# Layer 1 scans: a projection in two passes, copies on ScalarE instead of VectorE, and new costs for the order planner

## The chip, the cores and the metric

The kernel runs on one core of a Trainium2 chip. Five engines work beside each other[...]: TensorE (PE in the profile, PEld for its weight loads), VectorE (DVE), ScalarE (ACT), GpSimd (POOL) and SyncE (SP), which here issues all DMAs. [...] The metric is device time of one execution in microseconds (us), lower is better; the number compared is the median over runs.

## The reference

Two layers on x of shape (4, 128, 128, 192), float32. Each layer is x + block(groupnorm(x)). Layer 0's block has a state space scan with one state and dilated convolutions; it isn't touched here. Layer 1's block, cut to what matters:

```
xz = x @ in_proj_w;  x_ssm, z = halves          # C = 192
xc = silu(depthwise 3x3 conv(x_ssm) + conv_b)
xs = [xc row-major, reversed, column-major, reversed]      # K = 4 directions
proj  = xs @ x_proj_w[k]                        # 12 + 16 + 16 columns: dpart, B, C
delta = softplus(dpart @ dt_w[k] + 2 dt_b[k])
for t in 0 .. L-1:                              # L = 128 * 128
    state = exp(delta_t * A) * state + (delta_t * xs_t) * B_t      # 16 states a channel
    y_t   = sum over states of state * C_t
y = sum over k of (y_k + Ds * xs_k), each put back into image order
out = layernorm(y) * silu(z) @ out_w
```

The recurrence over 16,384 positions, for 4 images, 4 directions, 192 channels and 16 states, is most of the arithmetic. It is the part of the kernel that the change is in.

## The kernel before

The function `scans` handles two images at a time (a pair) as three blocks of 128 partitions: channels 0 to 127 of the first image, the last 64 channels of both, channels 0 to 127 of the second. Positions go in tiles of T = 1024. A *step* is one pair, one direction k and one tile: 2 x 4 x 16 = 128 steps. In a step there are six *groups* m of 64 channels (x = 0 to 5), and in a group eight *units* q, each of 64 channels times two states on 128 partitions: 48 units a step, 6,144 in all.

For one step, ahead of its scans:

- `load_u` (L1008) loads the three input blocks `u`.
- `project` makes `pj`, the columns dpart, B and C of both images, in two chunks of 512 positions. PE (L1028) sums three matmuls with 128 x 128 weights, one for each block i, into one PSUM bank; ScalarE copies it out (L1034); SP stores C for later (L1040).
- `step_sizes`, for each block i: two matmuls (L1051) and softplus on ScalarE (L1054) give delta, which goes to HBM (L1058); GpSimd multiplies it into u (L1061); PE transposes that (L1070), and a copy out of PSUM makes `dT` (L1076): on ScalarE for i = 0 and 1, on VectorE for i = 2.
- `diagonals`: for each of the step's two images and four quarters of the tile, two small matmuls transpose a piece of pj (L1094) and VectorE spreads it into a block-diagonal tile `D` (L1100).

For each unit:

- `fill`: eight matmuls (L1174) of 32-row tiles of dT with D make delta * u * B for all eight units of a group, an eighth of the positions at a time; ScalarE evicts them into the ring `H` of 18 slots (L1185). There is one fill buffer in PSUM.
- `unit`: ScalarE makes exp(delta * A) (`dA`, L1201, two buffers in PSUM); VectorE runs the recurrence with a scan instruction, in place in H (L1207); GpSimd multiplies by C (`hc`, L1213, three buffers); PE sums over the states with two 64-column matmuls that write the two halves of a bank (L1221).
- `finish`, after a group's eighth unit: ScalarE keeps the last state (L1237), and VectorE adds the sum to what the earlier direction left, or, for k = 2, which begins a new sum, only copies it out of PSUM (L1243, L1249; L1247 the copy). SP stores it (L1253).

All matmuls of `project`, `step_sizes` and `diagonals` share a single PSUM bank, tag `s`.

The order is not that of the loops. Every piece of work goes to `op(engine, cost, function, reads, writes, ...)` of the class `Order` (from L83). When all are known, `emit` plays them through with a list scheduler: each engine has a time at which it is free, each op a cost in us given by hand, a hop of 0.12 us between engines, 1.28 us for a ScalarE table switch, and DMAs at a given rate. It picks, again and again, the op that can start first; among those that can start within `idle` us of the engine's being free, it picks the one with the lowest rank. The rank is the op's place in the program less its `early`; an op that needs another ScalarE table has `keep` added. What comes out is written down as each engine's instruction order. On the chip the times are what they are; only the order is the planner's.

Of the kernel before, what the change touches and what calls it, by code (L numbers as in the profile page):

```python
# [12 lines left out]
ALU = mybir.AluOpType  # L13
# [187 lines left out]
class Maker:  # L201
# [741 lines left out]
    def scans(self, xc, delta, cs, y, w, ident, alog, dsum, dtb2):  # L943
# [22 lines left out]
        with ExitStack() as ctx:  # L966
# [11 lines left out]

            od = Order(window=3000, keep=1047, idle=0.500, rate=265e3)
            op = od.op  # L980
# [23 lines left out]
            def load_u(s):  # L1004
                p, k, at, j = steps[s]
                for i in range(3):
                    t = us[s, i] = buf("u", 3, 128, T)
                    op("SP", 0.1, lambda t=t, i=i: nc.sync.dma_start(  # L1008
                        t(), xc[k // 2][p][i][:, j * T : (j + 1) * T]
                    ), writes=[t], size=524e3, early=192)  # L1010
                if at == 0:
                    wt = buf("w", 2, 128, 2, 3, 128)
                    op("SP", 0.2, lambda: [
                        nc.sync.dma_start(wt()[:, 0], w["xp1"][:, k]),
                        nc.sync.dma_start(wt()[:, 1], w["dtw1"][:, k]),
                    ], writes=[wt], size=393e3, early=90)
                    wts[p, k] = wt

            def project(s):
                p, k, _, j = steps[s]  # L1020
                wt, uu = wts[p, k], [us[s, i] for i in range(3)]
                t = pj[s] = buf("pj", 1, 128, T)
                for c in range(2):
                    g = bank("P")

                    def mm(g=g, c=c):
                        for i in range(3):
                            nc.tensor.matmul(  # L1028
                                g(), wt()[:, 0, i], uu[i]()[:, 512 * c : 512 * c + 512],
                                start=(i == 0), stop=(i == 2),  # L1030
                            )

                    op("PE", 2.65, mm, reads=[wt, *uu], writes=[g], claims=[t])
                    op("ACT", 0.59, lambda g=g, c=c: nc.scalar.copy(  # L1034
                        t()[:, 512 * c : 512 * c + 512], g()), reads=[g, t], writes=[(t, c)])

                def store():
                    for e in range(2):
                        r = 64 * e + DR + NS
                        nc.sync.dma_start(cs[2 * p + e][k][:, j * T : (j + 1) * T], t()[r : r + NS])  # L1040

                op("SP", 0.2, store, reads=[(t, 0), (t, 1), t], writes=[("cs", s)], size=131e3)

            def step_sizes(s, i):

                p, k, _, j = steps[s]
                wt, u, x = wts[p, k], us[s, i], pj[s]
                l = buf("l", 3, 128, T)
                for c in range(2):
                    g = bank("P")  # L1050
                    op("PE", 0.9, lambda g=g, c=c: nc.tensor.matmul(  # L1051
                        g(), wt()[:, 1, i], x()[:, 512 * c : 512 * c + 512], start=True, stop=True,
                    ), reads=[wt, (x, c), x], writes=[g], claims=[l], early=-123)
                    op("ACT", 0.6, lambda g=g, c=c: nc.scalar.activation(  # L1054
                        l()[:, 512 * c : 512 * c + 512], g(), AF.Softplus,
                        bias=dtb2[:, i % 2, k : k + 1],
                    ), reads=[g], writes=[l], table="softplus")
                op("SP", 0.1, lambda: nc.sync.dma_start(  # L1058
                    delta[p][i][k][:, j * T : (j + 1) * T], l()
                ), reads=[l], writes=[("delta", s, i)], size=524e3)  # L1060
                op("POOL", 2.4, lambda: nc.gpsimd.tensor_tensor(u(), l(), u(), ALU.mult),  # L1061
                   reads=[l], writes=[u], early=30)
                t = dT[s, i] = buf("dT", 4, 128, 2, 8, 64)
                for c in range(2):
                    g = bank("P")

                    def mm(g=g, c=c):
                        for q in range(4):
                            b = 512 * c + 128 * q
                            nc.tensor.transpose(  # L1070
                                g()[:, 128 * q : 128 * q + 128], u()[:, b : b + 128], ident
                            )

                    op("PE", 0.95, mm, reads=[u], writes=[g], claims=[t], early=-249)
                    def turn(copy, g=g, c=c):
                        copy(  # L1076
                            t()[:, :, 4 * c : 4 * c + 4],
                            g().rearrange("t (q h c) -> t h q c", h=2, c=64),
                        )

                    if i < 2:
                        op("ACT", 0.6, lambda turn=turn: turn(nc.scalar.copy), reads=[g], writes=[t], early=-579)
                    else:
                        op("DVE", 0.69, lambda turn=turn: turn(nc.vector.tensor_copy),
                           reads=[g], writes=[t], early=-180)

            def diagonals(s, e, sb):
# [18 lines left out]

                op("PE", 0.4, mm, reads=[(x, sb // 2), x], writes=[g], claims=[t], early=-105)
                op("DVE", 1.2, spread, reads=[g], writes=[t], early=15)
                D[s, e, sb] = t
# [50 lines left out]
            def fill(m, sb, rp):  # L1160
# [19 lines left out]

                op("PE", 1.12, mm, reads=[td, tD], writes=[gs], claims=h[m])

# [8 lines left out]

                op("ACT", 1.13, evict, reads=[gs], writes=h[m])

            def unit(m, q):
# [5 lines left out]
                way = slice(None) if k % 2 == 0 else slice(None, None, -1)  # L1200
                op("ACT", 1.16, lambda: nc.scalar.activation(  # L1201
                    a(), d(), AF.Exp, scale=alog[:, c : c + 1]),
                    reads=[d], writes=[a], table="exp", early=-522)
                s0 = st.get((x, m - 6))

                def scan():
# [4 lines left out]

                op("DVE", 2.34, scan, reads=[a, *([s0] if at else [])], writes=[hq])
                op("POOL", 2.4, lambda: nc.gpsimd.tensor_tensor(t(), hs, tC(), ALU.mult),  # L1213
                   reads=[hq, tC], writes=[t])
                if q == 0:
# [9 lines left out]

                op("PE", 0.95, sum_n, reads=[t], writes=[ym], early=-252)

            def finish(m):
# [12 lines left out]
                def add():  # L1241
                    if k == 0:
                        nc.vector.scalar_tensor_tensor(  # L1243
                            t(), prev[m](), dsum[:, hf : hf + 1], ym(), ALU.mult, ALU.add
                        )
                    elif k == 2:
                        nc.vector.tensor_copy(t(), ym())  # L1247
                    else:
                        nc.vector.tensor_tensor(t(), prev[m](), ym(), ALU.add)  # L1249
# [4 lines left out]

                op("DVE", 0.72, add, reads=[ym, *([prev[m]] if k != 2 else [])], writes=[t])
                op("SP", 0.2, store, reads=[t], writes=[("y", p, k // 2, j, x)], size=262e3)
# [405 lines left out]
```

## Time and profile before

| | us |
|---|---|
| median of 3 runs | 26,409.49 (26,333.76 to 26,457.49) |
| the profiled execution | 26,512.26 |
| its span | 26,510.5 |
| of it, first to last scan of layer 1 | 17,697 (7,208 to 24,906) |

| engine | busy us | share of the span |
|---|---|---|
| PE matmul | 24,193.3 | 91% |
| DVE | 21,935.4 | 83% |
| ACT | 21,016.8 | 79% |
| POOL | 19,902.8 | 75% |

A row of the groups has the line, the engine, the operation, what it writes and reads, the shapes and the count; then the busy time and the mean duration in ns; then the time for which the engine stood idle just before such instructions and what ended most of that. The profile also records the clock that TensorE was granted (PEclk, 1.00 is full). The engines' shares are averages over stages with different limits, and matmul busy time is modelled.

### The profile page before, as it was taken

The page shows a single profiled execution, that of the slowest core. Times are in us where ns is not written, and L with a number is a line of the kernel's source. Part 1 is how long each engine was busy: PE and PEld are TensorE (multiplying, and loading weights), DVE is VectorE, ACT ScalarE, POOL GpSimd, SP SyncE. Part 2 cuts the span into 40 slices and gives each one's busy share as a digit, 9 for nine tenths or more (in the row PEclk, how much of TensorE's full clock was granted, in tenths as well). Part 3 has the DMA queues.
Part 4 walks back from the last instruction along what each step waited for, and adds up shares of the span by engine and source line. Part 5 has one row for each costly group of instructions (what it writes and reads, how often), then busy time and mean ns, then how long its engine had stood idle before and what let it go on. Part 6 is the DMA issues. An engine that isn't in the chain of part 4 may idle for free.

```text
span 26510.5 us, 438073 instructions
## 1 busy us (share of the span) xinstructions
PE 24193.3 (91%) x169220; PEld 9017.9 (34%) x169220; DVE 21935.4 (83%) x15401; ACT 21016.8 (79%) x24359; POOL 19902.8 (75%) x9450
## 2 busy tenths in 40 slices
PE   5999999998799999999999999999999999999699
PEld 3333333332233333333333333333333333333255
DVE  4888888888788889989898888888898888988643
ACT  5988898985588888888888888888888888888433
POOL 3777777763488888888888888888888888888400
PEclk7999999998899999999999899999899999999799
DMA  7999999995544444444444444444444444444573
GB/s 213 242 239 241 242 239 241 239 241 182 185 130 127 133 130 136 135 128 125 117 126 134 126 135 130 130 130 130 125 136 131 117 123 115 133 130 130 182 236 105
DMA packets 1667058, 4220.17 MB, mean 159 GB/s; under 512 B 238545, under 2 KB 387473, under 8 KB 1661905
## 3 DMA queue, kind: packets, MB, share of 16 engines
q1 hardware_dynamic: 1664976, 4192.14, 58.0%
q8 instruction: 1340, 21.95, 0.4%
q14 instruction: 742, 6.07, 0.1%
HBM read 3252.11 MB, written 939.10 MB: 158 GB/s over the span
## 4 chain that ended last, share of the span: by engine, by line
PE 40%; DVE 18%; ACT 11%; issue 6%; DMA 4%; POOL 3%; SPq 0%; DVEq 0%; POOLq 0%; ACTq 0%
DVE h L1207 14%; PE f L1174 13%; PE Y L1221 11%; ACT h L1185 6%; PE s L1028 3%; ACT dA L1201 3%; POOL hc L1213 2%; PE s L1051 2%; DMA C<-cs 2%; PE z L785 1%; PE hf L574 1%; DVE D L1100 1%; DVE acc L896 1%; PE f L785 1%; PE s L1094 1%
## 5 line engine op out<-in xcount | busy, mean ns | idle before, releaser
L1213 POOL TENSOR_TENSOR hc<-h,C 128x1024 f32<-128x1024 f32 x6144 | 14335.4, 2362 | 2412.5 <-PE Y L1221 1154.9
L1207 DVE TENSOR_TENSOR_SCAN h<-dA,st,h 128x1024 f32<-128x1024 f32 x5760 | 13130.9, 2331 | 779.9 <-ACT st L1237 290.6
L1185 ACT COPY h<-f 128x1024 f32<-128x1024 f32 (+3 forms) x8192 | 6332.9, 799 | 2256.1 <-PE f L1174 2185.0
L1174 PE MATMUL f<-D,dT 32*64 32x256 f32 x98304 | 7167.9, 408 | 777.5 <-ACT h L1185 633.6
L1221 PE MATMUL Y<-hc,sel 128*64 128x512 f32 x24576 | 7001.5, 657 | 475.1 <-POOL hc L1213 219.9
L1201 ACT ACTIVATE dA<-d,alog 128x1024 f32<-128x1024 f32 x6144 | 6905.9, 1124 | 301.6 <-DVE h L1207 247.2
L1174 PEld LDWEIGHTS f<-D,dT 32*64 32x64 f32 x98304 | 3279.1, 138 | 6688.2 <-ACT h L1185 4815.8
L452 POOL TENSOR_TENSOR xs<-xs,pr 128x1024 f32<-128x1024 f32 x1536 | 3637.3, 2371 | 329.2 <-ACT pr L447 249.4
L595 DVE SCALAR_TENSOR_TENSOR hf<-hh,vec,hf 128x512 f32<-128x512 f32 x3072 | 2317.8, 755 | 412.9 <-PE hf L574 272.7
L1221 PEld LDWEIGHTS Y<-hc,sel 128*64 128x64 f32 x24576 | 1322.6, 141 | 2979.6 <-issue 1811.3
L574 PE MATMUL hf<-sa,diag 96*32 96x512 f32 x18432 | 2152.3, 600 | 13.2 <-DMA sa<-hpad 11.3
L447 ACT ACTIVATE pr<-xi,vec 128x1024 f32<-128x1024 f32 x1536 | 1713.8, 1143 | 301.1 <-POOL xs L452 296.0
L1100 DVE TENSOR_TENSOR D<-s,mask 128x1024 f32<-128x1024 f32 x1024 | 1238.3, 1209 | 842.0 <-PE s L1094 842.0
L534 POOL TENSOR_TENSOR dl<-dl,xs 128x1024 f32<-128x1024 f32 x192 | 454.7, 2368 | 830.6 <-ACT dA L532 735.5
L574 PEld LDWEIGHTS hf<-sa,diag 96*32 96x32 f32 x18432 | 561.9, 109 | 1479.3 <-issue 1390.5
L1061 POOL TENSOR_TENSOR u<-l,u 128x1024 f32<-128x1024 f32 x384 | 907.2, 2363 | 163.4 <-ACT l L1054 136.0
L1207 DVE TENSOR_TENSOR_SCAN h<-dA,h 128x1024 f32<-128x1024 f32 x384 | 857.1, 2274 | 78.5 <-ACT dA L1201 45.3
L1051 PE MATMUL s<-pj,w 128*128 128x512 f32 x1536 | 892.3, 664 | 7.0 <-ACT l L1054 2.8
L1028 PE MATMUL s<-u,w 128*128 128x512 f32 x1536 | 756.4, 630 | 53.3 <-DMA prev<-xc 52.6
L1054 ACT ACTIVATE l<-s,vec 128x512 f32<-128x512 f32 x768 | 527.8, 687 | 328.5 <-PE s L1051 323.9
L1094 PEld LDWEIGHTS s<-ident,pj 128*128 128x128 f32 x4096 | 554.1, 196 | 599.5 <-issue 256.7
L392 PE MATMUL f<-xa,w 96*128 96x512 f32 (+1 forms) x1536 | 724.8, 616 | 25.7 <-ACT xi L407 25.5
(202 smaller groups left out, 21859.5 us busy)
## 6 DMA issues: line engine op xcount, KB each, us to landing
C<-cs SPq DMA_DIRECT2D x4096, 256.0 KB, 4.7
sa<-hpad SPq DMA_DIRECT2D x2304, 276.0 KB, 7.1
d<-delta SPq DMA_DIRECT2D x1536, 256.0 KB, 4.1
u<-xc SPq DMA_DIRECT2D x384, 512.0 KB, 4.6
delta<-l SPq DMA_DIRECT2D x384, 512.0 KB, 3.6
y<-y SPq DMA_DIRECT2D x1536, 128.0 KB, 3.2
hh<-hpad SPq DMA_DIRECT2D x384, 414.0 KB, 7.7
hpad<-hp SPq DMA_DIRECT2D x192, 552.0 KB, 7.2
```

Of the source, the lines that this page charges most:

```text
L447: op("ACT", 1.1, lambda pr=pr, t=t: nc.scalar.activation(rows(pr()), x()[:, t // 3 : t // 3 + R, t % 3 : t % 3 + W], AF.Copy, scale=v(k, V ...
L452: op("POOL", 2.38, lambda pr=pr: nc.gpsimd.tensor_tensor(o(), o(), pr(), ALU.add), reads=[pr], writes=[o], early=-429)
L574: nc.tensor.matmul(o()[32 * g : 32 * g + 32], diag[:, d, s, k, g], x[:, g, :, c0 : c0 + W], start=(d == 0 and s == 0), stop=(d == 1 and s ...
L595: nc.vector.scalar_tensor_tensor(o3, hh()[:, 1 + dy : 5 + dy, PAD + dx : PAD + dx + W], v(k, V0_K + col), o3, ALU.mult, ALU.add,)
L1028: nc.tensor.matmul(g(), wt()[:, 0, i], uu[i]()[:, 512 * c : 512 * c + 512], start=(i == 0), stop=(i == 2),)
L1100: nc.vector.tensor_tensor(t().rearrange("t a (n s) -> t (a n) s", s=32), g()[:, : 2 * NS].unsqueeze(2).to_broadcast([128, 2 * NS, 32]), ma ...
L1174: nc.tensor.matmul(gs()[64 * jn : 64 * jn + 64, n, 256 * a : 256 * a + 256], td()[rt, r // 64, 2 * sb + a], tD()[rt, a, 256 * jn : 256 * j ...
L1185: nc.scalar.copy(H[:, at : at + nq, 256 * sb : 256 * sb + 256].rearrange("p q (a r s) -> p q a r s", a=2, s=32)[:, :, :, 2 * rp : 2 * rp + 2],
L1201: op("ACT", 1.16, lambda: nc.scalar.activation(a(), d(), AF.Exp, scale=alog[:, c : c + 1]), reads=[d], writes=[a], table="exp", early=-522)
L1207: nc.vector.tensor_tensor_scan(hs[:, way], a()[:, way], hs[:, way], 0.0 if at == 0 else s0()[:, q : q + 1], ALU.mult, ALU.add,)
L1213: op("POOL", 2.4, lambda: nc.gpsimd.tensor_tensor(t(), hs, tC(), ALU.mult), reads=[hq, tC], writes=[t])
L1221: nc.tensor.matmul(ym()[64 * th : 64 * th + 64], sel, t()[:, 512 * th : 512 * th + 512], start=(q == 0), stop=(q == NQ - 1),)
```

## The change

Five things change, all in `scans`:

1. `project` issues, for each chunk, block 1's matmul with all 128 columns first, and then block 0's with columns 0 to 63 and block 2's with columns 64 to 127. Block 0 belongs to the first image and block 2 to the second, so the columns left out multiply by zero weights.
2. In `step_sizes`, the two copies to dT for block 2 go to ScalarE, as those of the other blocks do.
3. In `finish`, the copy for k = 2 goes to ScalarE.
4. The planner's costs are set anew (for instance L1221 from 0.95 to 1.09 us, L1051 from 0.9 to 1.1, the transposes from 0.95 to 1.16, the projection from 2.65 to 2.05), and `keep` and `idle` with them.
5. Many `early` values change: those of the u and weight loads are gone; scans now rank 255 later, exponentials 303 later (522 before), the fills 1,158 earlier, the products with C 1,329 earlier, and the spreads of D no longer 15 earlier.

The order of each of the five engines in this stage follows from all of these.

```diff
-            od = Order(window=3000, keep=1047, idle=0.500, rate=265e3)
+            od = Order(window=3000, keep=869, idle=0.400, rate=265e3)
...
                         t(), xc[k // 2][p][i][:, j * T : (j + 1) * T]
-                    ), writes=[t], size=524e3, early=192)
+                    ), writes=[t], size=524e3)
...
-                    ], writes=[wt], size=393e3, early=90)
+                    ], writes=[wt], size=393e3)
...
-                        for i in range(3):
+                        for i, m in ((1, slice(0, 128)), (0, slice(0, 64)), (2, slice(64, 128))):
                             nc.tensor.matmul(
-                                g(), wt()[:, 0, i], uu[i]()[:, 512 * c : 512 * c + 512],
-                                start=(i == 0), stop=(i == 2),
+                                g()[m], wt()[:, 0, i, m], uu[i]()[:, 512 * c : 512 * c + 512],
+                                start=(i == 1), stop=(i != 1),
                             )
-                    op("PE", 2.65, mm, reads=[wt, *uu], writes=[g], claims=[t])
+                    op("PE", 2.05, mm, reads=[wt, *uu], writes=[g], claims=[t])
...
-                    op("PE", 0.9, lambda g=g, c=c: nc.tensor.matmul(
+                    op("PE", 1.1, lambda g=g, c=c: nc.tensor.matmul(
...
-                    ), reads=[wt, (x, c), x], writes=[g], claims=[l], early=-123)
-                    op("ACT", 0.6, lambda g=g, c=c: nc.scalar.activation(
+                    ), reads=[wt, (x, c), x], writes=[g], claims=[l], early=-189)
+                    op("ACT", 0.69, lambda g=g, c=c: nc.scalar.activation(
...
-                    ), reads=[g], writes=[l], table="softplus")
+                    ), reads=[g], writes=[l], table="softplus", early=378)
...
-                op("POOL", 2.4, lambda: nc.gpsimd.tensor_tensor(u(), l(), u(), ALU.mult),
-                   reads=[l], writes=[u], early=30)
+                op("POOL", 2.38, lambda: nc.gpsimd.tensor_tensor(u(), l(), u(), ALU.mult),
+                   reads=[l], writes=[u])
...
-                    op("PE", 0.95, mm, reads=[u], writes=[g], claims=[t], early=-249)
+                    op("PE", 1.16, mm, reads=[u], writes=[g], claims=[t])
...
-                    if i < 2:
-                        op("ACT", 0.6, lambda turn=turn: turn(nc.scalar.copy), reads=[g], writes=[t], early=-579)
-                    else:
-                        op("DVE", 0.69, lambda turn=turn: turn(nc.vector.tensor_copy),
-                           reads=[g], writes=[t], early=-180)
+                    op("ACT", 0.6, lambda turn=turn: turn(nc.scalar.copy), reads=[g], writes=[t], early=-330)
...
-                op("PE", 0.4, mm, reads=[(x, sb // 2), x], writes=[g], claims=[t], early=-105)
-                op("DVE", 1.2, spread, reads=[g], writes=[t], early=15)
+                op("PE", 0.4, mm, reads=[(x, sb // 2), x], writes=[g], claims=[t], early=-168)
+                op("DVE", 1.2, spread, reads=[g], writes=[t])
...
-                op("PE", 1.12, mm, reads=[td, tD], writes=[gs], claims=h[m])
+                op("PE", 1.1, mm, reads=[td, tD], writes=[gs], claims=h[m], early=1158)
...
-                op("ACT", 1.13, evict, reads=[gs], writes=h[m])
+                op("ACT", 1.05, evict, reads=[gs], writes=h[m])
...
-                op("ACT", 1.16, lambda: nc.scalar.activation(
+                op("ACT", 1.13, lambda: nc.scalar.activation(
...
-                    reads=[d], writes=[a], table="exp", early=-522)
+                    reads=[d], writes=[a], table="exp", early=-303)
...
-                op("DVE", 2.34, scan, reads=[a, *([s0] if at else [])], writes=[hq])
-                op("POOL", 2.4, lambda: nc.gpsimd.tensor_tensor(t(), hs, tC(), ALU.mult),
-                   reads=[hq, tC], writes=[t])
+                op("DVE", 2.34, scan, reads=[a, *([s0] if at else [])], writes=[hq], early=-255)
+                op("POOL", 2.37, lambda: nc.gpsimd.tensor_tensor(t(), hs, tC(), ALU.mult),
+                   reads=[hq, tC], writes=[t], early=1329)
...
-                op("PE", 0.95, sum_n, reads=[t], writes=[ym], early=-252)
+                op("PE", 1.09, sum_n, reads=[t], writes=[ym], early=-270)
...
-                    elif k == 2:
-                        nc.vector.tensor_copy(t(), ym())
...
-                op("DVE", 0.72, add, reads=[ym, *([prev[m]] if k != 2 else [])], writes=[t])
+                if k == 2:
+                    op("ACT", 0.61, lambda: nc.scalar.copy(t(), ym()), reads=[ym], writes=[t])
+                else:
+                    op("DVE", 0.7, add, reads=[ym, prev[m]], writes=[t])
```

## The prediction

> **What bounds the kernel now.** I read the page first, then busy time by stretch, then the groups and the waits of the scans alone, then the timeline. The page's slices show that from slice 11 on four engines run at eight or nine tenths together:
>
> ```profile
> span 26510.5 us, 438073 instructions
> PE   5999999998799999999999999999999999999699
> DVE  4888888888788889989898888888898888988643
> ACT  5988898985588888888888888888888888888433
> POOL 3777777763488888888888888888888888888400
> ```
>
> The first scan begins at 7208 us and the last ends at 24906: 17,697 us for 128 steps, 138.3 each. The change touches nothing else, so the other 8,813 us stay.
>
> Which engine binds depends on the TensorE clock. Busy time by stretch (PE, PEld, DVE, ACT, POOL, clock, DMA share, GB/s), one stretch at full clock and one partly at half:
>
> ```profile
> 18000.00:18100.00 100.00, 92.71 (x776) 34.28 (x772) 93.24 (x49) 87.16 (x113) 89.59 (x39) 1.00 0.53 146
> 18100.00:18200.00 100.00, 97.75 (x563) 33.08 (x562) 66.83 (x35) 57.83 (x58) 57.98 (x26) 0.61 0.33 91
> ```
>
> At full clock VectorE is fullest. At half clock PE is, and everybody waits for it. By the trace's clock records the stage has 94 stretches at half clock, 2,034 us together. Of 127 whole steps, the 54 with a mean clock above 0.985 take 131.6 us, all together 138.2: the half clock costs 6.6 us a step, some 840 us. So this is a kernel bound by VectorE for 89% of the stage and by PE for 11%.
>
> VectorE's work per step, groups of the scans alone (busy, mean ns | idle before):
>
> ```profile
> L1207 DVE TENSOR_TENSOR_SCAN h<-dA,st,h 128x1024 f32<-128x1024 f32 x5760 | 13130.9, 2331 | 779.9 <-ACT st L1237 290.6 <-ACT dA L1201 255.6 <-ACT h L1185 170.2
> L1100 DVE TENSOR_TENSOR D<-s,mask 128x1024 f32<-128x1024 f32 x1019 | 1232.2, 1209 | 805.6 <-PE s L1094 805.6
> L1076 DVE COPY dT<-s 128x512 f32<-128x512 f32 x255 | 172.6, 677 | 91.0 <-PE s L1070 91.0
> L1247 DVE COPY y<-Y 128x512 f32<-128x512 f32 x192 | 129.5, 674 | 56.4 <-PE Y L1221 56.2
> ```
>
> Scans 13,988/128 = 109.3 (both scan groups), D 9.7, y 4.1, dT 1.35: 124.4 us of work in a full-clock step of 131.6. About 7 us are waits, and the largest is in the second line: VectorE stands 806 us (6.3 a step) before the spreading of D, for the small matmuls on L1094.
>
> [...] the half-clock stretches here last 3.4, 6.8, 17.1, 44.4, 51.2 or 78.5 us, whole windows. [...] PE was still busy 65% of the window before such a stretch (94 cases). [...] two 64-column matmuls of 512 columns take some 1.01 us[...].
>
> **The change part by part.**
>
> *Projection.* Each chunk issues a 128-column matmul and then two 64-column ones that write the two halves. Now (timeline):
>
> ```profile
> 15115.88 2.84 PE L1028 MATMUL s<-u,w 128*128 128x512 f32 x6
> 15118.66 1.09 PE L1174 MATMUL f<-D,dT 32*64 32x256 f32 x16
> ```
>
> Start to start 2.78 us for three, 0.92 each. After: 0.92 + 1.01 (a pair as in L1221) = 1.93, so 0.85 less for 256 chunks: 218 us of PE work. At full clock PE isn't the last, so that is hidden by VectorE's time. At half clock it counts double: 55 of the 94 stretches last until about the next projection, so about one chunk each runs slow, 55 x 1.7 = 94 us at most. I take 50. If the pair didn't run together, the gain is nothing.
>
> *dT copies of the third part.* 256 copies of 677 ns leave VectorE: -173 us. ScalarE gets 256 x 589 ns (its own dT row) = +151.
>
> *y copies of direction 2.* 192 x 674 ns leave VectorE: -129 us. ScalarE gets 192 x 587 ns (nearest row: dT of the same shape) = +113.
>
> VectorE's 302 us are worth their size where it binds, 89% of the stage: -268. ScalarE's 264 lie in its 23 us of idle time a step; without that cover they'd cost 264. The y copies wait for the last Y matmul of a group: by the order of the changed kernel they stand 2 to 4 dA exponentials behind that group's last, and the Y matmul ends a median of 7 us after its scan in this trace. Behind a waiting copy stand the fill evictions (PE waits for them) and the next dA (VectorE waits). From nothing to 1.5 us x 192 = 288; I take +60 with the rest of ScalarE's load.
>
> *Order.* The planner decides anew; table switches stay (764 to 768 loads). Moved: the projection goes from unit 19 of a step's 48 to unit 11; the step sizes go from exponentials 26, 38 and 2 of the next step to 26, 34, 42; SP's u loads and the second half of the D spreads move with them, the D of a step's later half from scans 16 to 20 to scans 10 to 13. The loads have whole units ahead of them, and the trace has PE waiting for a DMA before L1028 for 13 us in the stage. What matters is how far a D spread stands behind its matmul: counted in scans on VectorE minus Y pairs on PE, it was 2 to 9 and is now 2 (602 of 1024) or 3 (417). In the trace of before the spreads at 2, 3 and 4 waited 1.33, 1.40 and 1.04 us, those from 5 on 0.1 or less. So the new order could wait at all eight, 8 x 1.36 = 10.9 us a step. Against it, the old costs made PE too fast: L1221 at 0.95 against 1.08 in the timeline, L1051 at 0.9 against 1.12, so what was planned as ready came late; the new ones are at or above the trace (1.09, 1.10; L1070 1.16 against 0.66), so PE should come early. Bounds: nothing, or 10.9 us; I take the middle of 0 and 1.33 for eight, 5.2 a step against 6.3: -140 us over 128 steps.
>
> Sum: -268 - 50 - 140 + 60 = -398 us, against the profiled execution's 26,512. That one stands 0.4% above the median of 26,409; taken from the median it is 26,010, 1.5% less.
>
> **Rivals.**
>
> *The clock, for the worse (slower).* [...] at half clock a unit is fill then Y, 3.82 us in the timeline against 2.74 in a full-clock step (131.6/48)[...]. Before, no matmul of the s bank stands between units 3 and 19, and stretches that began at 3 or 4 lasted 51 to 78 us. In the new order that gap runs from unit 42 to 11 of the next step, some 17 units, right after a table switch in which ScalarE evicts hardly anything. One such stretch costs 17 x 1.08 = 18 us. Against the 398 gained it decides from 22 more of them in 128 steps; with one in every second step the end is 26,010 + 1,150 = 27,160, with 40 about 26,700. For it: stretches began beside such switches (units 3-4 and 37-38) 41 times. Against it: two sets of transposes stand at unit 41.
>
> *The clock, for the better.* The 34 stretches that begin at unit 12 of the old order need not recur, and the projection comes sooner to end others. Half of the 840 us gone: about 25,590.
>
> *The D spreads wait at every place.* 10.9 against 6.3 us: +590 instead of -140, so about 26,740.
>
> *The gain is swallowed.* Fill and eviction alternate over one buffer (PE's L1174 waits 4,810 us of weight-load time for L1185), and ScalarE gets 2.1 us a step more. If that loop sets the pace, VectorE's 302 us become idle time: 26,280 to 26,540.
>
> **How the numbers follow.** Likeliest 44%, 25,800 to 26,200 by itself; better clock 14%; swallowed 15%; worse clock 16%; D waits 11%. The measurement tells some 0.5% (132 us) from no change. Faster: 44 + 14 and 2 of the swallowed = 0.60; same 0.15 with the edges of two cases; slower 0.25. The range leaves out the end of the better clock and the worse half of the worse clock: 25,500 to 26,750.
>
> **What would show it.** Right: VectorE's L1076 and L1247 gone, L1028 near 1.9 us a chunk, idle time before D at or below 700 us, full-clock steps near 128 us, half-clock time near 2,000 us. Wrong: half-clock stretches of 50 us and more that begin at units 40 to 46; idle time before D over 1,200 us; new idle time of ScalarE before the y copies above 300 us, with VectorE's waits for dA above its 301.

## The result, and the profile after

The changed kernel takes 26,673.5 us, the kernel before 26,389.2 us (medians of 15 runs each): a ratio of 1.0104, with a 95% interval of 1.0077 to 1.0130. It is slower by 1%, where 1.5% faster was forecast. The two profiled executions show 124 us of these 284: before's lies 123 us above its own median, after's 37 below. What they show is therefore the direction of each part, and the sizes come from the runs. The granted clock is listed for every run: its median is 0.924 in the 15 runs of the changed kernel, and 0.944 to 0.945 in the runs of the kernel before that stood beside the experiments below.

The page of the kernel after, span, VectorE and granted clock by slice, and the clock row of the kernel before:

```profile
span 26634.2 us, 437801 instructions
DVE  4888888888789888888888888989999788889643
PEclk7999999998899888999889999999999888989799
```
```profile
PEclk7999999998899999999999899999899999999799
```

The clock row of the kernel after has 11 eights, that of the kernel before 4. By the clock records of the traces (173 of 0.5 and 173 of 1.0 in before, 188 of each in after, none between), the stage of the scans divides as follows. Stretches at half clock are counted in steps 2 to 127, where they begin; those of the first and the last step are left out. The *full-clock step* is the mean over the steps whose mean clock is above 0.985. Such a step can still hold one window of 3.4 us at half clock, so the table also has the *clean step*, the mean over steps with none at all. It is given for the directions 0, 1 and 3 together and for direction 2, since the moved y copies are in direction 2 only.

| | before | after |
|---|---|---|
| scan stage, us | 17,697 | 17,807 |
| full-clock step, us | 131.6 | 130.2 |
| clean step, directions 0, 1, 3, us (number) | 131.4 (36) | 130.1 (41) |
| clean step, direction 2, us (number) | 131.8 (15) | 129.6 (3) |
| stretches at half clock, number | 94 | 107 |
| half-clock time, us | 2,034 | 2,724 |

So at full clock the change did bring something: 1.4 us a step, 179 us over 128 steps. The half-clock time took more than that away. What one microsecond at half clock costs comes from (stage - 128 x full-clock step) / half-clock time: 0.42 in both kernels, and between 0.35 and 0.49 in the twelve experiments below. 690 us more at 0.42 is about 290 us lost, by this estimate.

The groups of the kernel after that answer to those shown of before (busy, mean ns | idle before and what ended it), the scans of layer 1 alone:

```profile
L1203 DVE TENSOR_TENSOR_SCAN h<-dA,st,h 128x1024 f32<-128x1024 f32 x5760 | 13136.2, 2334 | 958.2 <-ACT dA L1197 447.6 <-ACT st L1233 304.4 <-ACT h L1181 189.3
L1096 DVE TENSOR_TENSOR D<-s,mask 128x1024 f32<-128x1024 f32 x1019 | 1243.2, 1220 | 1046.7 <-PE s L1090 1034.3
L1076 ACT COPY dT<-s 128x512 f32<-128x512 f32 x764 | 459.9, 602 | 0.1
L1250 ACT COPY y<-Y 128x512 f32<-128x512 f32 x192 | 112.0, 583 | 21.4 <-PE Y L1217 20.3
```

Both kinds of copies are on ScalarE and wait for next to nothing there. VectorE is rid of them, and its idle time over the stage is larger: before the scans 958 us (780 before), before the spreads of D 1,047 us (806 before).

These sums mix full and half clock, and what they seem to say is wrong for full clock. In clean steps of the directions 0, 1 and 3 the idle time before D *fell*, from 5.7 to 3.7 us a step; that before the scans stayed (3.1 and 2.9); the adds of y on VectorE now wait 1.7 us, where they waited 0.1. In direction 2 the wait before D rose from 5.6 to 7.0 us and that before the scans from 3.4 to 4.8. About four fifths of the 1,047 us lie in steps with half-clock time.

The projection runs as predicted. The timeline of the changed kernel at full clock has the six records of one chunk's three matmuls start to next start in 1.96 us, against 2.78 before:

```profile
7412.98 2.13 PE L1028 MATMUL s<-u,w 128*128 128x512 f32 x6
7414.94 1.89 PE L1217 MATMUL Y<-hc,sel 128*64 128x512 f32 x8
```

Now where the clock falls. In the kernel after, 46 of the 107 stretches begin at scan unit 5 (while VectorE is at the fifth scan of a step) and last 27 to 51 us, nearly all between 41 and 48: 1,984 us of the 2,724. One of them, busy time in three windows of 3.41 us in a row (PE, PEld, DVE, ACT, POOL, clock, DMA share, GB/s):

```profile
15095.87:15099.29 3.42, 3.23 (x38) 1.22 (x36) 3.42 (x3) 2.56 (x4) 1.58 (x2) 1.00 0.99 256
15099.29:15102.70 3.41, 2.00 (x22) 0.71 (x20) 3.41 (x2) 3.29 (x6) 3.41 (x2) 0.99 0.08 25
15102.70:15106.11 3.41, 3.26 (x22) 1.09 (x20) 3.41 (x3) 2.43 (x5) 3.41 (x3) 0.50 0.00 0
```

PE is busy for 2.00 of 3.41 us in the middle one, which makes it thin, and in the next the clock is 0.50. The timeline of that place:

```profile
15098.21 1.09 PE L1170 MATMUL f<-D,dT 32*64 32x256 f32 x16 [0.19 <-ACT h L1181]
15098.72 11.62 POOL L1209 TENSOR_TENSOR hc<-h,C 128x1024 f32<-128x1024 f32 x5 [1.84 <-DVE h L1203]
...
15100.71 1.09 PE L1170 MATMUL f<-D,dT 32*64 32x256 f32 x16 [1.41 <-ACT h L1181]
...
15101.73 1.12 PE L1217 MATMUL Y<-hc,sel 128*64 128x512 f32 x4
...
15103.00 1.98 PE L1170 MATMUL f<-D,dT 32*64 32x256 f32 x16
```

Two fills follow each other on PE with no Y pair between. The second waits 1.41 us for the eviction of the first, since there is one fill buffer, and in that time PE has nothing. No product `hc` is ready there: VectorE has just done two instructions that aren't scans (y and a spread of D), and GpSimd idled 1.84 us for it. That the planner put the fills so for the same reason is likely, but not shown. The new order has this pair 120 times, after the second Y pair of a step; the old one has 112 such pairs after the eighth, where 34 stretches begin at scan unit 12.

What stands at the end of a stretch differs too. In the old order two Y pairs stand in a row on PE, the 13th and 14th of the step, in 112 steps. 30 of the 34 stretches end with them after 17 us, five units ahead of the projection, which stands behind the 19th pair. The chain of work of the kernel before has the end of the stretch that began at 15085.02 (the clock is back at 15102.08):

```profile
15097.33 1.91 PE f L1174 x16
15099.25 3.29 PE Y L1221 x8
15102.54 1.02 PE f L1174 x16
```

In the new order nothing of the kind stands between the second Y pair and the projection, which stands behind the 11th or 12th: no two Y pairs in a row, but for two steps, and no matmul of the s bank longer than those of D. 45 of the 46 stretches last until the projection. In the one shown, PE issues ten fills, eight Y pairs and three sets of D's matmuls up to there, 3.82 us for a fill with its Y pair:

```profile
15103.00:15146.00 43.00, 42.83 (x228) 14.71 (x228) 27.03 (x15) 21.53 (x26) 23.76 (x11) 0.53 0.10 25
15146.00:15170.00 24.00, 22.79 (x197) 7.73 (x198) 23.08 (x11) 21.63 (x32) 21.80 (x10) 1.00 0.66 162
```

PE is full for 42.83 of 43.00 us, everybody else waits for it, and the clock is back at 15143.60, 3.1 us after the start of the projection at 15140.51.

### The profile page after: what moved, and what is told of

Read it like the earlier page. It is cut to its first block, busy times and chain, and to the rows that moved or that the text cites. A ratio compares the mean times of both kernels' runs of the same rounds, so it can differ in the third digit from the quotient of the medians.

```text
span 26634.2 us, 437801 instructions
## 1 busy us (share of the span) xinstructions
PE 24355.6 (91%) x169220; PEld 9018.5 (34%) x169220; DVE 21731.1 (82%) x14953; ACT 21187.7 (80%) x24811; POOL 19904.0 (75%) x9450
## 4 chain that ended last, share of the span: by engine, by line
PE 38%; ACT 25%; DVE 10%; issue 6%; DMA 2%; POOL 1%; SPq 0%; DVEq 0%; ACTq 0%; POOLq 0%
PE f L1170 16%; ACT h L1181 12%; DVE h L1203 7%; ACT dA L1197 7%; PE Y L1217 7%; PE s L1028 2%; PE s L1051 2%; PE s L1090 1%; PE z L785 1%; PE hf L574 1%; ACT l L1054 1%; ACT dT L1076 1%; DVE D L1096 1%; ACT L1054 1%; ACT L1197 1%
## 5 line engine op out<-in xcount | busy, mean ns | idle before, releaser
L1170 PE MATMUL f<-D,dT 32*64 32x256 f32 x98304 | 7321.9, 415 | 845.9 <-ACT h L1181 666.0
L1051 PE MATMUL s<-pj,w 128*128 128x512 f32 x1536 | 873.8, 651 | 163.7 <-ACT l L1054 162.3
L660 PE MATMUL g<-xz,w 96*128 96x512 f32 x1536 | 724.7, 607 | 18.8 <-DVE y L653 18.7
L896 DVE SCALAR_TENSOR_TENSOR acc<-xi,vec,acc 128x1024 f32<-128x1024 f32 x384 | 715.2, 1863 | 26.9
```

What stands on the lines that cost most here:

```text
L1051: op("PE", 1.1, lambda g=g, c=c: nc.tensor.matmul(g(), wt()[:, 1, i], x()[:, 512 * c : 512 * c + 512], start=True, stop=True,), reads=[wt, ...
L1170: nc.tensor.matmul(gs()[64 * jn : 64 * jn + 64, n, 256 * a : 256 * a + 256], td()[rt, r // 64, 2 * sb + a], tD()[rt, a, 256 * jn : 256 * j ...
```

## The experiments

All keep the order of either kernel as its planner makes it, and edit what is issued in it, except where it says otherwise. The steps and the half-clock time are of the profiled execution of each run, which lies within 50 us of the run's median but for e2 (150 us below), e3 (82 below) and e7 (113 above). Clean steps are those of the directions 0, 1 and 3, with their number; before has 131.4, after 130.1.

| run | full-clock step | clean step (number) | half-clock us | median us | ratio to before (95%) |
|---|---|---|---|---|---|
| e1 after, extra matmul | 130.3 | 130.0 (41) | 1,000 | 25,869 | 0.9777 (0.9753-0.9801) |
| e2 before, extra matmul | 131.7 | 131.5 (71) | 843 | 26,187 | 0.9900 (0.9871-0.9928) |
| e3 after, three passes | 132.1 | 131.3 (9) | 4,342 | 27,528 | 1.0416 (1.0389-1.0442) |
| e4 before, two passes | 131.2 | 131.1 (44) | 2,068 | 26,469 | 1.0019 (1.0002-1.0036) |
| e5 after, tiny matmul | 130.2 | 130.0 (49) | 2,505 | 26,438 | 1.0010 (0.9995-1.0025) |
| e6 e1, D spreads later | 131.3 | none | 2,884 | 26,880 | 1.0173 (1.0154-1.0193) |
| e7 e1, copies back | 132.2 | 130.9 (16) | 3,130 | 26,825 | 1.0156 (1.0132-1.0179) |
| e8 new work, old planner values | 131.7 | 131.7 (36) | 2,959 | 26,888 | 1.0178 (1.0159-1.0197) |
| e9 after, two matmuls at unit 8 | 133.1 | 131.0 (2) | 2,321 | 26,710 | 1.0118 (1.0093-1.0142) |
| e10 e1, more matmuls | 130.0 | 130.0 (79) | 734 | 25,782 | 0.9756 (0.9735-0.9777) |
| e11 e1, old work | 133.6 | 132.5 (18) | 2,273 | 26,757 | 1.0131 (1.0112-1.0151) |
| e12 e2, two passes | 131.2 | 131.0 (55) | 1,242 | 26,147 | 0.9892 (0.9856-0.9929) |

**Is it the thin window? More work for PE.** Theory: the loss is the clock, released by the gap between two fills. Rival: the new order stalls, and the clock only follows. The two say opposite things of one more matmul in that gap. Its output goes into columns of the s bank's current tile that nothing reads.

```diff
+                    if kind[a] == kind[b] == "fill" and bank is not None:   # a, b: neighbours on PE
+                        found[b] = lambda g=bank: nc.tensor.matmul(         # issued before b
+                            g()[:, 128:512], ident, warm_in[:, 128:512], start=True, stop=True
+                        )
```

> The changed kernel in its own order, with one more matmul (128 x 128 weights, 384 columns, result unused) between the two fills that follow each other on PE without a Y pair, once a step, 120 in all. Clock theory: the 46 half-clock stretches that begin at unit 5 (1,984 us) are released by the thin window at these two fills; with the gap filled they go, half-clock time falls from 2,724 us to below 1,200, and at 122 us of step time per unit of clock or 0.28 us per us of half clock the median falls by 555 to 870 us, to 25,800 to 26,120. Order theory (the loss is stalls of the new order, the clock only follows): 120 x 0.75 us more work on a PE that is 91% busy, so 26,670 to 26,770 and half-clock time as before.

25,869 us: 3.2% less than the changed kernel (0.9777 / 1.0104) for 120 matmuls more. The group of stretches at unit 5 is gone, half-clock time is 1,000 us, and the full-clock step is what it was (130.3). The timeline shows the gap, filled:

```profile
14954.14 1.09 PE L1173 MATMUL f<-D,dT 32*64 32x256 f32 x16
...
14955.16 0.91 PE L1271 MATMUL s<-warm_in,ident 128*128 128x384 f32 x2
...
14956.61 1.09 PE L1173 MATMUL f<-D,dT 32*64 32x256 f32 x16 [0.54 <-ACT h L1184]
```

And the stretch of 43 us behind it, against that of the changed kernel above, has the clock at 0.96 and VectorE busy for 40.66 us where it was 27.03:

```profile
14956.00:14999.00 43.00, 39.55 (x341) 14.22 (x340) 40.66 (x22) 34.75 (x38) 36.21 (x17) 0.96 0.19 50
```

The same in the kernel before, at its own pair of fills:

> The kernel before with the same extra matmul between its own two fills in a row (unit 8 of Y, where 34 half-clock stretches of 691 us in all begin, at scan unit 12). Clock theory: these 34 go, 195 to 300 us less, about 26,090 to 26,200; those at units 3 and 4 (1,062 us) stay. Order theory: no change, or up to 90 us more.

26,187 us, 1.0% less. The 34 stretches at unit 12 are gone, and some at units 3 and 4 remain (584 us; the profiled execution is a quick one). So both kernels carry the same fault in different places.

**Is it the work in the gap, or any disturbance?** The control has the same instruction in the same place, with 16 columns instead of 384.

```diff
-                            g()[:, 128:512], ident, warm_in[:, 128:512], start=True, stop=True
+                            g()[:, 128:144], ident, warm_in[:, 128:144], start=True, stop=True
```

> Control for the extra matmul: same place, same count and weights, but 16 columns in place of 384, so the same order and the same waits with hardly any work. Clock theory: the window stays thin, half-clock time stays near the changed kernel's 2,724 us (2,200 to 3,200), median 26,550 to 26,800. Rival (any shift of a step's phase against the clock's windows, or the extra instruction's waits, is what helped): near 25,870 as with 384 columns.

26,438 us: 235 us less than the changed kernel, below the expected bracket, with 2,505 us of half clock, of which 1,698 still begin at unit 5 (39 stretches). 570 us of the gain need the columns. That 235 come without them wasn't expected. The clean step is the same (130.0), and the granted clock has a median of 0.935 over 22 runs, against 0.924 over 15 of the changed kernel. That is some 620 us less at half clock, about 250 us at 0.4, so this part is half-clock time too; why there is less of it isn't settled.

**Can a stretch be ended early?** Two such matmuls at unit 8, with the gap at the fills left alone.

```diff
+                    if kind[a] == "unit" and kind[b] == "fill" and pairs % 48 == 8 and bank is not None:
+                        found[b] = lambda g=bank: [nc.tensor.matmul(
+                            g()[:, 128:512], ident, warm_in[:, 128:512], start=True, stop=True
+                        ) for _ in range(2)]
```

> The changed kernel in its own order, thin window left as it is, but two 384-column matmuls (result unused) between Y pair and fill at unit 8 of every step, three units after the half-clock stretches begin and three before the projection. Clock theory: about as many stretches begin at unit 5 as in the changed kernel (46, or up to 60), but they end within 10 to 24 us in place of 41 to 48, half-clock time 1,300 to 2,000 us, median 26,150 to 26,450. Rival (the extra work only moves the phase of the steps): stretches as long as before, 41 us and more, and the median at 26,600 or above.

The stretches do end early: 40 begin at unit 5, and all 40 end after 23.9 or 27.3 us, within 1.4 us of the end of the two matmuls. 32 of them come in the time expected, the other eight a little later. The timeline shows the two matmuls at half clock (2.93 us for four records), and behind them the fill is already faster:

```profile
12143.68 1.98 PE L1220 MATMUL Y<-hc,sel 128*64 128x512 f32 x4
12145.58 2.93 PE L1273 MATMUL s<-warm_in,ident 128*128 128x384 f32 x4
12148.44 1.34 PE L1173 MATMUL f<-D,dT 32*64 32x256 f32 x16
12149.71 1.08 PE L1220 MATMUL Y<-hc,sel 128*64 128x512 f32 x4
```

The time doesn't: 26,710 us. 90 stretches now begin at units 13 and 14, for a reason that isn't settled; 23 of the 25 steps behind the 133.1 us hold one window of half clock. PE has no gap here to hide the two matmuls in, and the two clean steps take 131.0 us, 1.0 more than those of the changed kernel. Preventing the stretches left the clean step as it was (e1); ending them did not.

**What is each part of the change worth in its own order?** The projection first.

```diff
-                        for i, m in ((1, slice(0, 128)), (0, slice(0, 64)), (2, slice(64, 128))):
+                        for i in range(3):
                             nc.tensor.matmul(
-                                g()[m], wt()[:, 0, i, m], uu[i]()[:, 512 * c : 512 * c + 512],
+                                g(), wt()[:, 0, i], uu[i]()[:, 512 * c : 512 * c + 512],
```

> The changed kernel in its own order with the projection in three full passes again, nothing else. If the two-pass projection brings what was predicted: 0.85 us x 256 more on PE, at full clock mostly hidden, so 0 to 100 us slower than the changed kernel, 26,670 to 26,770. If the two-pass form is what spoils the clock (less dense work to end a half-clock stretch): faster than the changed kernel by more than 100 us and shorter stretches from unit 5.

> The kernel before in its own order with the two-pass projection alone. As predicted: L1028 from 2.78 to 1.93 us a chunk, 0 to 100 us faster than before, 26,290 to 26,390. If a less dense projection lengthens half-clock stretches: slower than before, with more half-clock time than 2,034 us.

Both expectations of e3 missed, and the median of e4 lies 80 us above its bracket. Three passes in the new order lengthen the clean step by 1.2 us (131.3 against 130.1), of the 2 x 0.82 that they take on PE. The full-clock step grows by 1.9, but 16 of e3's 36 full-clock steps hold a window of half clock. The median rises by 854 us, mostly because 86 stretches instead of 46 begin at unit 5: half-clock time grows by 1,618 us, some 680 at 0.42. In the old order two passes save 0.4 us a step, clean or not, and the median doesn't fall (1.0019). So at full clock three quarters of the projection's time were hidden in the old order, and one quarter in the new.

The copies, moved back at the matching places of the same order:

```diff
-                    op("ACT", 0.6, lambda turn=turn: turn(nc.scalar.copy), reads=[g], writes=[t], early=-330)
+                    way = nc.vector.tensor_copy if i == 2 else nc.scalar.copy
+                    op("ACT", 0.6, lambda turn=turn, way=way: turn(way), reads=[g], writes=[t], early=-330)
...
+                for n in new:                       # on VectorE behind the scan that stands there
+                    ops[n] = ("DVE", *ops[n][1:])
```

> The changed kernel with the 384-column matmuls, and 446 of the 448 moved copies (dT of block 2, y of direction 2) back on VectorE, at the matching places of the same order. As predicted (VectorE binds at full clock): 302 us of work more, full-clock steps 2.1 us longer, median 26,080 to 26,180. If the saving is swallowed by waits: 25,850 to 25,950.

Clean steps are 0.9 us longer than e1's (130.9 against 130.0). They are all of the directions 0, 1 and 3, where only the dT copies were moved, 1.35 us a step: two thirds of VectorE's work is found again in the step. The full-clock step grows by 1.8, near the 2.1 expected, but by accident: 52 of its 68 steps hold a window of half clock, and none is of direction 2, where the y copies are. So no run measures what the y copies alone bring. None of the 32 steps of direction 2 runs at full clock here, and they take 162 us each. The median is off the bracket, since half-clock time went to 3,130 us.

For direction 2 there is only the whole change: its clean steps fell from 131.8 us to 129.6 (129.7 in e1, 13 steps). VectorE has 5.4 us less to do in them, so more than half of that doesn't reach the step.

Then both back, which leaves the new order with the old work:

> The order of the changed kernel with the 384-column matmuls, but the work of before: three full passes in the projection and 446 copies back on VectorE. It measures what the order alone costs while the clock is full. If the parts add up (three passes +1.9 us a step, copies +1.8, measured in this order): full-clock steps of 133.5 to 134.5 us, so the new order costs 2 to 3 us a step more than the old one (131.6) for the same work. If the two overlap: about 132.2, and the order costs nothing to speak of. The median depends on where half-clock stretches fall: with some 3,000 us of them, as with the copies back alone, about 27,050.

133.6 us, within the expected bracket, but again 46 of the 64 steps hold a window of half clock. Clean steps take 132.5 us, 2.5 more than e1's, so the parts nearly add up (1.2 and 0.9 by themselves). For the same work the new order needs 1.1 us more a clean step than the old one (131.4). VectorE waits 4.0 us before D, where it waited 5.7, and 1.8 before the adds of y, where it waited 0.1; all its waits together come to 9.4 us and to 9.2, so for most of the 1.1 us the traces name no wait. The median is below the expected one with the shorter half-clock time.

The other way round, the new work under the planner values of before (here the planner decides anew):

```diff
-                        for i in range(3):
+                        for i, m in ((1, slice(0, 128)), (0, slice(0, 64)), (2, slice(64, 128))):
...
-                        op("DVE", 0.69, lambda turn=turn: turn(nc.vector.tensor_copy),
-                           reads=[g], writes=[t], early=-180)
+                    op("ACT", 0.6, lambda turn=turn: turn(nc.scalar.copy), reads=[g], writes=[t], early=-579)
...
+                if k == 2:
+                    op("ACT", 0.61, lambda: nc.scalar.copy(t(), ym()), reads=[ym], writes=[t])
```

> The kernel before with the two-pass projection and both kinds of copies moved to ScalarE, under its old costs and ranks (0.61 us for the moved y copy); the planner decides anew. In its order two fills in a row without a Y pair come up 42 times, shortly before the projection, not 112 times. If the new costs and ranks are what places the thin window: less half-clock time than before's 2,034 us, full-clock steps of 129 to 131 us, median 25,950 to 26,250. If moving the work itself thins PE: slower than before.

Missed on both sides. Clean steps take 131.7 us, no less than before's 131.4, though VectorE has 1.35 us less to do in them and PE 1.6 less, and half-clock time is 2,959 us. Counting the pairs of fills didn't foretell it: 25 stretches of 1,168 us begin at unit 11, where the order has no such pair, so a stretch can begin without such a pair.

**Do the waits before the D spreads matter?** The 602 spreads that stand two scans behind their matmul, each behind one scan more:

```diff
+                        if scans_done - after_y[b] == 2:
+                            held.append(n)          # re-issued after the next scan
```

> The changed kernel with the 384-column matmuls, and the 602 spreads of D that stand two scans behind their matmul moved one scan later on VectorE, nothing else. If waits before the spreads swallowed VectorE's saving: idle time before D falls from 634 us to below 250 and full-clock steps from 130.3 to 127 to 129 us, median 25,500 to 25,750. If they only show where VectorE waits for a PE that is behind anyway: the idle time moves to the scans, full-clock steps stay at 130 to 131 us, median 25,800 to 25,950.

Idle time before D falls to 447 us, and that before the scans rises from 770 to 1,859:

```profile
L1247 DVE TENSOR_TENSOR_SCAN h<-dA,st,h 128x1024 f32<-128x1024 f32 x5760 | 13210.3, 2336 | 1707.7 <-ACT dA L1241 1120.1 <-ACT st L1277 368.9 <-ACT h L1225 184.6
L1140 DVE TENSOR_TENSOR D<-s,mask 128x1024 f32<-128x1024 f32 x1019 | 1229.0, 1206 | 447.3 <-PE s L1134 447.1
```

Part of that rise is half-clock time, 2,884 us against 1,000. Only nine steps ran at full clock, all clean and of direction 2, with 131.3 us against 129.7 in e1. In these the wait before D fell from 6.9 to 2.9 us a step and that before the scans rose from 4.4 to 10.0. The waits moved, and the step didn't get shorter. The median is worse because new stretches arose: 58 at unit 44 and 80 at unit 14, 1,800 us. So to shorten the waits before D by itself brings nothing, in direction 2 at least; for the others e6 has no clean step.

**A version that beats both.** e1 with the extra matmul also where two fills have only matmuls of D between them, 219 in all:

```diff
-                    if kind[a] == kind[b] == "fill" and bank is not None:
+                    if kind[b] == "fill" and set(since) <= {"diagonals"} and bank is not None:
```

> The changed kernel with the 384-column matmul also where two fills have only the small matmuls of D between them (99 more, at unit 11, where windows are thin too and stretches begin at unit 13 and 14: 279 us in the run with 120). Clock theory: these go, half-clock time from 1,000 to about 750 us, median 25,750 to 25,850. Rival: stretches there last only until the projection just behind them, so nothing is won and 99 x 0.75 us lost: 25,870 to 25,950.

25,782 us, 2.4% less than before, with 99 of 127 steps at full clock. The stretches at units 13 and 14 are gone but one. And the kernel before with both of its own remedies:

> The kernel before in its own order with the two-pass projection and the 384-column matmul between its own two fills in a row. If both gains stand beside each other: 0.4 us a step under the kernel before with the extra matmul alone (26,187), about 26,100 to 26,180, half-clock time below 1,200 us. If the thinner projection costs clock again: 26,190 to 26,350 with more half-clock time than the 843 us of that run.

26,147 us as expected; half-clock time is somewhat over the bound given. With extra matmuls the changed kernel is 2.4% below before, and the old order with two passes 1.1%. Of the 365 us between e10 and e12 some 160 are the full-clock step, 1.2 us shorter, and some 210 the half-clock time, 508 us less. The change was a gain hidden under a larger loss.

## Why the prediction was wrong

**Which engine binds.** At half clock it held: PE is busy for 42.83 of 43.00 us in the stretch shown, VectorE for 27.03. At full clock it held in part: in the new order 1.35 us of VectorE's work are worth 0.9 us of a clean step (e7), and 1.64 us of PE's are worth 1.2 (e3), so a step hangs on both engines. To reckon full and half clock apart was right; half-clock time was priced at 840 us for 2,034, which is 0.41 each, and the runs give 0.35 to 0.49.

**The copies.** The dT copies were put at 1.35 us a step and bring 0.9. The y copies were put at 4.0 in each step of direction 2; there the whole change brings 2.2 of the 5.4 us that leave VectorE, so the rival that the gain is swallowed came true in part. The +60 for ScalarE was too much: the y copies wait 21 us in all.

**The projection.** The size held (1.93 predicted, 1.96 measured). Its worth did not: "hidden by VectorE's time" is largely true of the old order (0.4 us a step) and false of the new, where it is worth 1.2 us a clean step. A chunk at half clock does take about twice its time: 3.91 us against 1.97 in after (medians of 13 and 176 chunks, start to next start), 5.42 against 2.77 in before (one and 239). But the 50 us rest on a misreading: of the 55 stretches said to last until about the next projection, 15 do. The other 40 end at the two Y pairs in a row, five units earlier.

**The order: the step that failed first.** I gave it -140 us and counted only the waits before D. These did fall in clean steps, to 4.5 us on average over the directions, where 5.2 was forecast; most of the stage's 1,047 us come from steps with half-clock time. What failed is that all else that a new order does was put at nothing. The runs show +1.1 us a clean step for the same work (e11 against before), some 140 us the other way if direction 2 is like the others; the new waits of the adds of y are one thing that comes with it. The rival that D waits at every place, at 10.9 us a step, didn't come: 7.0 at most.

**The clock: the step that decided.** The sum left half-clock time as it was. The dT copies and the projection together are worth 2.5 us a clean step (e11 against e1), the order takes 1.1 back, and 1.4 were measured, 179 us in all; half-clock time rises by 690 us, some 290. I had named it as the rival on the other side, at 16%, and rightly expected long stretches between units 42 and 11: 45 of the 46 that begin at unit 5 last until the projection, 41 us and more. But I hadn't seen that 43 of the 94 stretches of before end with two Y pairs in a row, and that the new order has no such pairs in that gap. The trigger was wrong as well: I had looked for it beside the table switches, at unit 42, where 6 stretches begin. It lies at the two fills in a row, which the order of the changed kernel shows and which, in the trace of before, stood just ahead of the 34 stretches at unit 12. I had counted those 34 and put them down as something that need not recur. What PE did in the window before one of them would have told what to look for in the new order. None of the three signs that were to show the forecast wrong came up.

**Left open.** Why direction 2 holds most of the half-clock time in the changed kernel (144.3 us a step, 136.6 to 138.1 in the others) and in e7. Of the 17 pairs of neighbouring steps that both have a stretch at unit 5, 8 have them 153.6 us apart and 7 have 150.2, 45 and 44 windows of 3.413. What sets these distances isn't settled. Nor is it settled where e8's stretches at unit 11 come from, why e9 has so many at unit 13, what the y copies alone bring, and where most of the order's 1.1 us lie.

## What to carry to other kernels

Before judging a new order, split the time by the granted TensorE clock: here it is two kernels, one in which VectorE and PE share the step and one bound by PE, and a gain in the one was lost by more of the other. Compare steps without any half clock, and of the same kind of work: a mean that lets in single windows of half clock gave 1.8 us for copies that are worth 0.9. In the order of each kernel, look for the place where PE is thin (61% busy on average before the stretches at unit 5) and for the work at which the clock comes back. Here 45 of the 46 stretches at unit 5 lasted from the one to the other, the projection, 41 to 51 us. Where PE had a gap anyway, a matmul whose result nobody reads was worth 3%.

## What the runs showed of the hardware

The figures are those of the traces of before and after, steps 2 to 127, unless a run is named. All 94 and 107 stretches at half clock begin on one grid of 3.4133 us in each trace, to within 0.004 us, and last whole multiples of it (3.4 to 78.5 us in before, 3.4 to 116.1 in after), while the steps take anything from 129 to 166 us.

In the window of 3.41 us before a stretch PE was far from idle: busy for 65% of it on average in before (53 to 80%) and for 66% in after (52 to 83%), for 61% before the 46 stretches at unit 5, with no gap over 1.7 us. Windows at full clock that full clock followed have 91% in both traces. A window with so little work wasn't always followed by half clock: 33 windows of before and 57 of after have PE busy for less than 65% and are followed by full clock.

PE was busy all through long stretches without the clock coming back: for 98% of the 21 stretches over 40 us in before, and for 99.6% of the 47 in after. In the one shown it had fills and Y pairs in turn, with the small matmuls of D, 42.83 of 43.00 us. At half clock a fill takes 1.91 us, start to next start, where it takes 1.02 at full clock (medians, the same in both traces).

Stretches end with windows that hold mostly other matmuls than fills: 43 of the 94 in before end with the two Y pairs in a row (3.29 us in the chain above), 62 of the 107 in after with the projection, and the 40 at unit 5 of e9 within 1.4 us of the end of the two added 128 x 128 matmuls (2.93 us in the timeline above). In the last window of a stretch fills take 16% of the time in before and 13% in after, in the windows ahead of it 49% in both. What it is of PE's work that decides the clock, no run here shows.
